# Preparing the last batch element's attention of a two-layer graph kernel: three blocks of Wh and half of the maxima moved beside the normalizing of its last block

## The chip, the cores and the metric

The kernel runs on one core of one Trainium2 chip. The metric is the device time of one execution in microseconds (us), the median of several runs. The profiled execution is one more run, with its own time and its own span.

## The reference, cut to what matters

Two layers run one after the other on x, of shape (8, 2048, 256) in float32, with one 2048 x 2048 adjacency matrix.

- Layer 0 is attention with four heads over chunks of 256 keys: scores are clipped to -10 to 10, masked with the adjacency, and each chunk has its own softmax. Its output is projected, added to x and normalized, and the result is added to x and normalized again. Call that h.
- Layer 1 is graph attention: Wh = h W, s_i = Wh a1, s_j = Wh a2, e = leaky_relu(s_i + s_j) with slope 0.2, masked by the adjacency, a softmax over all 2048 keys, then the sum of Wh with these weights, an ELU, the addition of h and a normalization.

```python
s_i = Wh @ a1
s_j = Wh @ a2
e = jax.nn.leaky_relu(s_i[:, :, None] + s_j[:, None, :], negative_slope=LEAKY_ALPHA)
e = jnp.where(mask[None, :, :], e, -jnp.inf)
attention = jax.nn.softmax(e, axis=-1)
h_prime = jnp.einsum('bij,bjo->bio', attention, Wh)
```

The layer-1 softmax of a query needs the largest score among its neighbours before any weight of that query can be made. As the slope is positive, it is enough to know the largest s_j among the neighbours.

## The kernel before, in words

The program is one instruction stream per engine, in an order written out by hand. The eight batch elements are run one after the other through layer 0, each in four blocks of 512 queries (IB = 512, NIB = 4), and each block in eight chunks of 256 keys (NCH = 8). The outer loop runs over all of these chunks (index J); each J has two halves, and each half is a **beat**. There are total = B * NIB * NCH = 256 chunks, so the loop's last score is made in beat 511, and beats 512 and 513 finish its products. Batch elements are numbered 0 to 7, and (7,3) is the last block of the last one. After the loop a short loop of its own goes on with beats until nothing is left (lines 782 to 786). This stretch is the **tail**.

A beat has three parts:

- begin_beat takes the layer-1 steps onward. A step is 128 keys against the 512 queries of one block; a block has 16 steps, a batch element four blocks. A step is *low* on ScalarE (L524) in one beat, *leaky* (L528) and *edges* (L533, with the mask) on VectorE in the next, *weights* (the exp, L537, on ScalarE, and for all but the last batch element an accumulate on GpSimd, L544 and L546) and *product* (TensorE, L556, or L571 for the last batch element) in the one after. A credit decides how many steps begin in a beat: 1.5 in the loop, 1.1 for its last batch element, 1.0 in the tail. The steps come strictly in order, so a batch element's first step cannot begin before the last step of the batch element ahead of it.
- Scores and context products of layer 0 stand in the middle. The last scaling of a context (L750 on VectorE, L751 on GpSimd) comes two beats after the product that it belongs to.
- end_beat issues the products, and then resumes each generator of two lists once: `ahead` (the preparation of layer 1, function prelude) and `fins` (fin after a layer-0 block, fin1 after a layer-1 block). Each `yield` ends a generator's turn in that beat.

fin normalizes a block of layer 0 over some ten beats: x loaded; two GpSimd additions; three beats later the output projection (L331), VectorE's addition (L338) and the first statistics (L292 to L295, and a power on GpSimd, L296); L301 and L303 normalize; GpSimd multiplies and adds (L343, L344); second statistics; second normalizing and the store of h; transposes (L356) into hT, which is stored too. For the last block of the last batch element, (7,3), the context is complete in beat 514, the projection is in beat 515, the second statistics in 518 and the transposes in 520. fin1 of the block of layer 1 ahead of it runs in the same beats (L486 and L487 in 519, its statistics in 520).

prelude(b) waits until all four blocks of batch element b have been normalized, loads hT back, makes Wh in one beat per block (L391 on TensorE, L394 on ScalarE), takes the columns s_j and s_i (L399 to L401), turns s_j into a row and spreads it over all partitions through DRAM (L406 to L412), and then makes the maxima. `far` is a matrix in DRAM, made at the start, that is 0 for a neighbour and hugely negative elsewhere. For each 128 queries and each half of the keys, L432 on VectorE adds s_j and a block of far (128 x 1024, 256 KB, loaded by L420 through two buffers) and takes the maximum: 32 such instructions per batch element. After eight of them, five small operations (L446 to L450) make the bounds for a block of 512 queries, which are transposed and spread through DRAM (L453 to L463). A block may start two beats after that.

All DMAs are issued by SP in one stream; an SP instruction that waits for a buffer holds back those behind it. The last batch element's Wh and key row use the buffers of kT and v, which layer 0 no longer needs. The product of the last batch element's layer 1 lies in the two PSUM buffers of the scores (ps_s).

Of the kernel before, what the change touches and what calls it, by code (L numbers as in the profile page):

```python
# [9 lines left out]
F32 = mybir.dt.float32  # L10
BF16 = mybir.dt.bfloat16
# [3 lines left out]
ALU = mybir.AluOpType  # L15
# [4 lines left out]
P = 128  # L20
CLIP = 10.0
EPS = 1e-5
SLOPE = 0.2
FAR = -(2.0**127)
# [4 lines left out]
def tile_adj_attention__then__gat(  # L29
# [35 lines left out]
    nc = tc.nc  # L65
    B, N, F = x.shape
    H, D = 4, 64
    CHUNK = 256
    KC = F // P
    NT = N // P  # L70
    IB = 512
    NIB = N // IB
    TPB = IB // P
    NPAIR = H // 2
    NCH = N // CHUNK
    DH = D // 2
    HT = NT // 2
    HN = N // 2
# [4 lines left out]
    dram3 = ctx.enter_context(tc.tile_pool(name="dram3", bufs=3, space=DRAM))  # L83
    ps_s = ctx.enter_context(tc.tile_pool(name="ps_s", bufs=2, space=PSUM))
    ps_u = ctx.enter_context(tc.tile_pool(name="ps_u", bufs=1, space=PSUM))
    ps_m = ctx.enter_context(tc.tile_pool(name="ps_m", bufs=2, space=PSUM))
    one = ctx.enter_context(tc.tile_pool(name="one", bufs=1))
    two = ctx.enter_context(tc.tile_pool(name="two", bufs=2))
    three = ctx.enter_context(tc.tile_pool(name="three", bufs=3))
    four = ctx.enter_context(tc.tile_pool(name="four", bufs=4))  # L90
# [221 lines left out]
    fin_near = [0] * B  # L312
    fins = []

    def fin(b, ib, ctxT):
# [37 lines left out]
        for k in range(KC):  # L353
# [1 line left out]
            for t in range(TPB):  # L355
                nc.tensor.transpose(pt[:, t, :], y[:, t, ts(k, P)], ident)  # L356
            nc.scalar.copy(hT[:, k, :], pt.rearrange("p t c -> p (t c)"))
        nc.sync.dma_start(out=hT_d[b, ib], in_=hT)


    blocks_done = 0

    def prelude(b):

        st = states[b]
        last = b == B - 1
        while fin_near[b] < NIB:
            yield  # L370
        hts = []

        def ht_load():
            ib = len(hts)
            if ib < NIB:
                t = four.tile([P, KC, IB], F32, tag="xT", name=f"hTl{b}_{ib}")
                nc.sync.dma_start(out=t, in_=hT_d[b, ib])
                hts.append(t)

        ht_load()  # L380
        ht_load()
        yield
        yield
        while not (last or blocks_done == b * NIB):
            yield
        wh = one.tile([P, NT, F + 2], F32, tag="kT" if last else "wh", name=f"wh{b}")
        for ib in range(NIB):
            for t in range(TPB):
                pw = ps_m.tile([P, F + 2], F32, tag="m", name=f"pw{b}_{ib}_{t}")
                for k in range(KC):  # L390
                    nc.tensor.matmul(  # L391
                        pw, hts[ib][:, k, ts(t, P)], W_aug[:, k, :], start=(k == 0), stop=(k == KC - 1)
                    )
                nc.scalar.copy(wh[:, ib * TPB + t, :], pw)  # L394
            ht_load()
            yield

        sj = two.tile([P, 3, NT], F32, tag="sj", name=f"sj{b}")
        nc.vector.tensor_copy(sj[:, 0, :], wh[:, :, F + 1])  # L399
        nc.vector.tensor_scalar_mul(sj[:, 1, :], wh[:, :, F + 1], SLOPE)  # L400
        nc.vector.tensor_copy(sj[:, 2, :], wh[:, :, F])  # L401
        if last:
            nc.vector.memset(wh[:, :, F : F + 1], 1.0)
        yield
        pt = ps_m.tile([NT, P], F32, tag="m", name=f"psj{b}")
        nc.tensor.transpose(pt, sj[:, 0, :], ident)  # L406
        rows = two.tile([NT, P], F32, tag="rows", name=f"sjr{b}")
        nc.scalar.copy(rows, pt)
        sj_d = dram3.tile([NT, P], F32, tag="sj_d", name=f"sj_d{b}")
        nc.sync.dma_start(out=sj_d, in_=rows)  # L410
        sj_row = one.tile([P, N], F32, tag="v" if last else "sj_row", name=f"sj_row{b}")
        nc.sync.dma_start(out=sj_row, in_=sj_d.rearrange("r c -> (r c)").partition_broadcast(P))  # L412
        st["wh"], st["sj"] = wh, sj
        fbs = []

        def fb_load():
            n = len(fbs)
            if n < 2 * NT:
                fb = two.tile([P, HN], BF16, tag="fb", name=f"fb{b}_{n}")
                nc.sync.dma_start(out=fb, in_=far[n // 2, n % 2])  # L420
                fbs.append(fb)

        fb_load()
        fb_load()
        yield
        yield
        for ib in range(NIB):

            mx = two.tile([P, TPB], F32, tag="mx", name=f"mx{b}_{ib}")
            m2 = two.tile([P, 2, TPB], F32, tag="m2", name=f"m2{b}_{ib}")  # L430
            for n in range(2 * TPB):
                nc.vector.tensor_tensor_reduce(  # L432
                    out=fbs[2 * TPB * ib + n],
                    in0=sj_row[:, ts(n % 2, HN)],
                    in1=fbs[2 * TPB * ib + n],
                    scale=1.0,
                    scalar=2 * FAR * 0.999,
                    op0=ALU.add,
                    op1=ALU.max,
                    accum_out=m2[:, n % 2, n // 2 : n // 2 + 1],  # L440
                )
                fb_load()
                if ib or n % 2:
                    yield
            s_i = sj[:, 2, ts(ib, TPB)]
            nc.vector.tensor_max(mx, m2[:, 0, :], m2[:, 1, :])  # L446
            nc.vector.tensor_add(mx, mx, s_i)
            nc.vector.scalar_tensor_tensor(mx, mx, SLOPE, mx, ALU.mult, ALU.max)
            nc.vector.tensor_sub(m2[:, 0, :], s_i, mx)
            nc.vector.scalar_tensor_tensor(m2[:, 1, :], s_i, SLOPE, mx, ALU.mult, ALU.subtract)  # L450
            yield
            pt = ps_m.tile([2 * TPB, P], F32, tag="m", name=f"pab{b}_{ib}")
            nc.tensor.transpose(pt, m2.rearrange("p n t -> p (n t)"), ident)  # L453
            rows = two.tile([2 * TPB, P], F32, tag="rows", name=f"abr{b}_{ib}")
            nc.scalar.copy(rows, pt)
            ab_d = dram3.tile([2 * TPB, P], F32, tag="ab_d", name=f"ab_d{b}_{ib}")
            nc.sync.dma_start(out=ab_d, in_=rows)
            yield

            while blocks_done < b * NIB + ib - 1:  # L460
                yield
            ab = two.tile([P, 2, IB], F32, tag="ab", name=f"ab{b}_{ib}")
            nc.sync.dma_start(  # L463
                out=ab.rearrange("p n q -> p (n q)"),
                in_=ab_d.rearrange("r c -> (r c)").partition_broadcast(P),
            )
            st["ab"][ib] = (beat + 2, ab)

    def fin1(b, ib, hx, acc):

# [25 lines left out]
            nc.scalar.activation(hx[:, t, :], us[t], AF.Identity, bias=ones[:, 0:1], scale=r[:, t : t + 1])  # L496

    states = [{"ab": {}} for _ in range(B)]

    def layer1():  # L500

# [89 lines left out]

    l1 = layer1()
    l1_live = True
    ahead = [prelude(b) for b in range(B)]
    lows, edged, weighted = [], [], []
    agenda = {}
    beat = 0
# [35 lines left out]
    def end_beat():  # L633

        nonlocal weighted
        for s in weighted:
            s.product()
        weighted = []
        for gens in (ahead, fins):
            for g in list(gens):  # L640
                if next(g, g) is g:
                    gens.remove(g)
        for fn in agenda.pop(beat, []):
            fn()
# [13 lines left out]

    prev = None
    v = None  # L660
    total = B * NIB * NCH
    mk0 = {}
    for J in range(total + 1):
        b, ib, j = J // (NIB * NCH), J // NCH % NIB, J % NCH
# [166 lines left out]
```

## Time and profile before

| what | value |
| --- | --- |
| median of 3 runs | 4443.78 us (4443.62 to 4454.05) |
| profiled execution, own time | 4445.93 us |
| its span | 4444.1 us |
| TensorE busy | 4076.1 us (92%) |
| VectorE busy | 3405.3 us (77%) |
| ScalarE busy | 2603.7 us (59%) |
| GpSimd busy | 1776.4 us (40%) |
| DMA over the span | mean 98 GB/s |
| span from the last scores' end to the kernel's end | about 4140 to 4444 us |

How to read it: the span is the time from the first to the last instruction of the profiled execution; shares are averages over stages with different limits. PE is TensorE, PEld its weight loads, DVE VectorE, ACT ScalarE, POOL GpSimd, SP the engine that issues DMAs. PEclk is the granted clock of TensorE as a share of full speed. A row such as "L432 ... 1.22" is a duration, and what stands in square brackets is the idle time of that engine ahead of the instruction and what ended it. A VectorE row that is longer than its fellows of the same shape was held up while it ran.

### The profile page before, as it was taken

What the parts mean: (1) busy time and instruction counts of PE and PEld (TensorE: products, weight loads), DVE (VectorE), ACT (ScalarE), POOL (GpSimd) and SP (SyncE); (2) the same over time, 40 slices, a digit from 0 to 9 for tenths busy, and PEclk for the clock granted to TensorE, in tenths of its full rate; (3) what the DMA queues carried; (4) which work ended last, traced back from release to release, by engine and by line L of the source; (5) the groups of instructions that cost most, each with busy time, mean ns of one, the idle gap of its engine ahead of it and who ended that gap; (6) DMA issues with size and microseconds to landing.
All of it is one profiled execution on the core that took longest, in us unless ns stands there. A gap on an engine that the chain in (4) does not pass through costs nothing. (4 is left out here: it accounts for less than half of the span.)

```text
span 4444.1 us, 61341 instructions
## 1 busy us (share of the span) xinstructions
PE 4076.1 (92%) x23052; PEld 1914.3 (43%) x23052; DVE 3405.3 (77%) x4527; ACT 2603.7 (59%) x3877; POOL 1776.4 (40%) x906
## 2 busy tenths in 40 slices
PE   7888999999899998999999999999989999899767
PEld 3222334444344543445334453444434444344545
DVE  4777469985799758996599866998579975898686
ACT  4665445665556655665556655666555665566445
POOL 0222224553355423554345542455325553355411
PEclk9999999999999999999999999999999999999988
DMA  4554333332322323323333223332232232332241
GB/s 149 167 164 152 92 100 101 96 93 78 105 81 91 101 64 115 89 77 92 99 99 91 78 77 104 101 101 86 84 101 87 86 103 68 118 92 73 65 136 54
DMA packets 266874, 433.98 MB, mean 98 GB/s; under 512 B 86097, under 2 KB 121169, under 8 KB 265553
## 3 DMA queue, kind: packets, MB, share of 16 engines
q1 hardware_dynamic: 266576, 430.06, 31.7%
q8 instruction: 181, 2.97, 0.3%
q14 instruction: 117, 0.95, 0.1%
HBM read 358.48 MB, written 69.40 MB: 96 GB/s over the span
## 5 line engine op out<-in xcount | busy, mean ns | idle before, releaser
L702 ACT ACTIVATE e<-sc 128x1024 f32<-128x1024 f32 x1024 | 1037.3, 1022 | 1146.7 <-DVE sc L699 1102.2
L699 DVE SCALAR_TENSOR_TENSOR sc<-sc,mk 128x1024 f32<-128x1024 f32 x1024 | 1205.8, 1222 | 512.8 <-PE sc L689 282.9
L689 PE MATMUL sc<-qT,kT 64*128 64x512 f32 x4096 | 1060.0, 632 | 106.9 <-ACT e L702 104.0
L751 POOL TENSOR_TENSOR ctxT<-ctxT,un 128x1024 f32<-128x1024 f32 x224 | 562.7, 2512 | 1164.1 <-DVE un L750 1059.1
L715 PE MATMUL u<-e,v 128*32 128x512 f32 x8192 | 980.4, 596 | 0.0
L556 PE MATMUL us<-wh,w 128*128 128x256 f32 x3584 | 875.5, 393 | 78.1 <-ACT w L537 60.5
L556 PEld LDWEIGHTS us<-wh,w 128*128 128x128 f32 x3584 | 662.8, 192 | 420.7 <-ACT w L537 117.7
L546 POOL TENSOR_TENSOR acc<-acc,w 128x512 f32<-128x512 f32 x392 | 602.7, 1537 | 541.0 <-ACT w L537 531.3
L689 PEld LDWEIGHTS sc<-qT,kT 64*128 64x128 f32 x4096 | 346.1, 188 | 627.4 <-ACT e L702 307.4
L528 DVE SCALAR_TENSOR_TENSOR w<-ab,sj,w 128x512 f32<-128x512 f32 x512 | 584.0, 1161 | 32.1 <-ACT w L524 32.1
L715 PEld LDWEIGHTS u<-e,v 128*32 128x32 f32 x8192 | 239.8, 110 | 657.7 <-issue 539.2
L533 DVE TENSOR_TENSOR w<-w,mk 128x512 f32<-128x512 f32 x512 | 475.1, 948 | 44.4 <-DMA mk<-mask 41.7
L715 PE MATMUL u<-e,ones 128*32 128x512 f32 x4096 | 498.3, 604 | 0.0
L432 DVE CUSTOM_DVE_ANT_0 fb<-sj_row,fb 128x1024 bf16<-128x1024 f32 x256 | 397.1, 1559 | 5.9 <-DMA fb<-far 5.6
L537 ACT ACTIVATE w<-w 128x512 f32<-128x512 f32 x512 | 310.7, 631 | 90.0 <-DVE w L533 89.6
L524 ACT ACTIVATE w<-ab,sj 128x512 f32<-128x512 f32 x512 | 353.3, 716 | 13.5 <-PE us L571 6.3
L750 DVE TENSOR_TENSOR un<-un,r 128x1024 f32<-128x1024 f32 x224 | 276.5, 1234 | 85.4 <-DMA r<-rd 78.8
L723 ACT COPY un<-u 128x512 f32<-128x512 f32 x512 | 300.6, 587 | 55.4 <-PE u L715 53.7
L715 PEld LDWEIGHTS u<-e,ones 128*32 128x32 f32 x4096 | 107.9, 110 | 359.5 <-issue 317.9
L737 DVE RECIPROCAL dc<-dc 128x16 f32<-128x16 f32 x256 | 64.1, 250 | 184.5 <-DMA dc<-ds 159.7
L571 PE MATMUL us<-wh,w 128*128 128x257 f32 x512 | 128.7, 413 | 45.9 <-ACT w L537 45.7
L487 POOL TENSOR_TENSOR hx<-hx,hr 128x1024 f32<-128x1024 f32 x32 | 91.6, 2862 | 191.6 <-DVE hx L486 191.6
(97 smaller groups left out, 3150.7 us busy)
## 6 DMA issues: line engine op xcount, KB each, us to landing
r<-rd SPq DMA_DIRECT2D x256, 256.0 KB
fb<-far SPq DMA_DIRECT2D x256, 256.0 KB
mk<-mask SPq DMA_DIRECT2D x120, 512.0 KB
xT_k<-in_xT_dram SPq DMA_DIRECT2D x32, 512.0 KB
raw<-in_adjT_dram SPq DMA_DIRECT2D x32, 512.0 KB
xT_q<-in_xT_dram SPq DMA_DIRECT2D x32, 512.0 KB
rawf<-in_adj_dram SPq DMA_DIRECT2D x32, 512.0 KB
xT_v<-in_xT_dram SPq DMA_DIRECT2D x32, 512.0 KB
```

The costliest lines, as they stand in the source:

```text
L432: nc.vector.tensor_tensor_reduce(out=fbs[2 * TPB * ib + n], in0=sj_row[:, ts(n % 2, HN)], in1=fbs[2 * TPB * ib + n], scale=1.0, scalar=2 * ...
L524: nc.scalar.activation(self.w, k["ab"][:, 1, :], AF.Identity, bias=k["sj"][:, 1, c : c + 1])
L528: nc.vector.scalar_tensor_tensor(self.w, k["ab"][:, 0, :], k["sj"][:, 0, c : c + 1], self.w, ALU.add, ALU.max)
L533: nc.vector.tensor_tensor(self.w, self.w, self.k["mks"][self.c // HT][:, self.c % HT, :], ALU.min)
L537: nc.scalar.activation(self.w, self.w, AF.Exp)
L546: nc.gpsimd.tensor_add(k["acc"], k["acc"], self.w)
L556: nc.tensor.matmul(k["us"][:, t, :], self.w[:, ts(t, P)], k["wh"][:, c, 0:F], start=(first and t % 2 == 0), stop=last, skip_group_check=True,)
L689: nc.tensor.matmul(sc[:, h, :], kT[h * D : (h + 1) * D, hp, ts(c, P)], qT[h * D : (h + 1) * D, hp, :], start=True, stop=True,)
L699: nc.vector.scalar_tensor_tensor(scs[hp], scs[hp], -CLIP, cap, ALU.max, ALU.min)
L702: nc.scalar.activation(e, scs[hp], AF.Exp)
L715: nc.tensor.matmul(m[h * DH : (h + 1) * DH, :], prev["v"][:, pc, f0 : f0 + DH] if part < 2 else ones[:, 0:DH], prev["es"][2 * i + h // 2][ ...
L751: nc.gpsimd.tensor_add(p["ctxT"], p["ctxT"], p["un"])
```

## The change

For batch elements 0 to 6 the preparation issues the same instructions as before; it is only cut into functions. For the last one a generator of its own, last_prelude, takes its place:

- At beat 2*total - 4 (508) it loads hT of the three blocks that are ready.
- In beats 512, 513 and 514 it makes Wh of these three blocks. In 513 it also takes the key columns of the first half (blocks 0 and 1); in 514 it spreads their row and loads far for eight of the sixteen groups of 128 queries whole, 512 KB each, into the eight buffers of the layer-0 exponentials (tag "e"), which are free by then.
- In beats 515 to 519 it issues three maxima a beat over the first half of the keys, until fin has made the last hT.
- In beat 520 it makes Wh of the last block straight from fin's tile (which is no longer stored and loaded back), the key columns and the row of the second half. The sixteenth maximum over the first half and those over the second half follow, four of them in one beat for block 0, then one a beat. Groups 8 to 15 come through the two far buffers as before.
- A block may start one beat after its bounds are spread, where it was two.
- From beat 2*total on, end_beat resumes fins before ahead.

```diff
-        nc.sync.dma_start(out=hT_d[b, ib], in_=hT)
+        if (b, ib) == (B - 1, NIB - 1):
+            states[b]["hT"] = hT
+        else:
+            nc.sync.dma_start(out=hT_d[b, ib], in_=hT)
...
+    def key_columns(wh, sj, r):
+        nc.vector.tensor_copy(sj[:, 0, r], wh[:, r, F + 1])
+        nc.vector.tensor_scalar_mul(sj[:, 1, r], wh[:, r, F + 1], SLOPE)
+        nc.vector.tensor_copy(sj[:, 2, r], wh[:, r, F])
+
+    def key_rows(b, sj, sj_row, r):
+        n = r.stop - r.start
+        pt = ps_m.tile([n, P], F32, tag="m", name=f"psj{b}_{r.start}")
+        nc.tensor.transpose(pt, sj[:, 0, r], ident)
+        rows = two.tile([n, P], F32, tag="rows", name=f"sjr{b}_{r.start}")
+        nc.scalar.copy(rows, pt)
+        sj_d = dram3.tile([n, P], F32, tag=f"sj_d{n}", name=f"sj_d{b}_{r.start}")
+        nc.sync.dma_start(out=sj_d, in_=rows)
+        nc.sync.dma_start(
+            out=sj_row[:, r.start * P : r.stop * P], in_=sj_d.rearrange("r c -> (r c)").partition_broadcast(P)
+        )
...
+    def last_prelude(b):
+        st = states[b]
+        while beat < 2 * total - 4 or fin_near[b] < NIB - 1:
+            yield
+        hts = [load_hT(b, ib) for ib in range(NIB - 1)]
+        while beat < 2 * total:
+            yield
+        wh = one.tile([P, NT, F + 2], F32, tag="kT", name=f"wh{b}")
+        sj = two.tile([P, 3, NT], F32, tag="sj", name=f"sj{b}")
+        wh_block(b, wh, hts[0], 0)
+        yield
+        wh_block(b, wh, hts[1], 1)
+        halves = [slice(0, HT), slice(HT, NT)]
+        key_columns(wh, sj, halves[0])
+        yield
+        sj_row = one.tile([P, N], F32, tag="v", name=f"sj_row{b}")
+        key_rows(b, sj, sj_row, halves[0])
+        wh_block(b, wh, hts[2], 2)
+        held = []
+        for it in range(HT):
+            fr = eight.tile([P, N], BF16, tag="e", name=f"far{b}_{it}")
+            nc.sync.dma_start(out=fr.rearrange("p (n w) -> p n w", n=2), in_=far[it].rearrange("n p w -> p n w"))
+            held.append(fr)
+        fbs, fb_load = far_loads(b, [(it, hf) for hf in range(2) for it in range(HT, NT)])
+        yield
+        m2 = one.tile([P, NIB, 2, TPB], F32, tag="m2l", name=f"m2{b}")
+
+        def half(it, hf):
+            fb = held[it][:, ts(hf, HN)] if it < HT else fbs.pop(0)
+            half_max(sj_row, fb, hf, m2[:, it // TPB, hf, it % TPB : it % TPB + 1])
+            if it >= HT:
+                fb_load()
+
+        firsts = list(range(NT))
+        while "hT" not in st:
+            for it in firsts[:3]:
+                half(it, 0)
+            firsts = firsts[3:]
+            yield
+        wh_block(b, wh, st["hT"], NIB - 1)
+        key_columns(wh, sj, halves[1])
+        nc.vector.memset(wh[:, :, F : F + 1], 1.0)
+        key_rows(b, sj, sj_row, halves[1])
+        st["wh"], st["sj"] = wh, sj
+        yield
+        while firsts:
+            half(firsts.pop(0), 0)
+        for ib in range(NIB):
+            for t in range(TPB):
+                half(ib * TPB + t, 1)
+                if ib:
+                    yield
+            less_max(sj, ib, m2[:, ib], f"{b}_{ib}")
+            ab_d = query_rows(m2[:, ib], f"{b}_{ib}")
+            yield
+            while blocks_done < b * NIB + ib - 1:
+                yield
+            st["ab"][ib] = (beat + 1, query_bc(ab_d, f"{b}_{ib}"))
...
-    ahead = [prelude(b) for b in range(B)]
+    ahead = [prelude(b) for b in range(B - 1)] + [last_prelude(B - 1)]
...
-        for gens in (ahead, fins):
+        for gens in (ahead, fins) if beat < 2 * total else (fins, ahead):
```

wh_block, load_hT, far_loads, half_max, less_max, query_rows and query_bc hold the instructions of lines 387 to 467 unchanged.

## The prediction

> **What bounds the kernel now.** Read first: the page's 40 slices. TensorE fills 0.9 of nearly every slice; only the last three are slack, and in two of them the granted clock drops too.
>
> ```profile
> PE   7888999999899998999999999999989999899767
> DVE  4777469985799758996599866998579975898686
> PEclk9999999999999999999999999999999999999988
> ```
>
> A slice is 111 us, so this is from about 4111 us on. All that the change moves lies there; before beat 508 it issues the same instructions. Second: busy time by stage, cut at the landmarks of that tail.
>
> ```profile
> core 0: us, PE busy (x) PEld busy (x) DVE busy (x) ACT busy (x) POOL busy (x), PEclk, DMA share, GB/s
> 4140.30:4155.40 15.10, 10.99 (x50) 7.60 (x50) 14.28 (x9) 5.04 (x10) 12.66 (x6) 0.89 0.32 87
> 4155.40:4185.90 30.50, 16.62 (x65) 13.56 (x64) 20.88 (x34) 13.34 (x23) 17.58 (x11) 0.78 0.11 36
> 4185.90:4221.40 35.50, 26.80 (x115) 21.36 (x113) 14.64 (x27) 15.42 (x34) 9.01 (x7) 0.95 0.25 88
> 4221.40:4233.50 12.10, 9.53 (x41) 7.41 (x41) 7.32 (x6) 5.45 (x10) 7.05 (x5) 1.00 0.37 133
> 4233.50:4250.20 16.70, 8.26 (x24) 5.54 (x24) 15.94 (x21) 2.50 (x4) 4.58 (x3) 0.76 0.36 110
> 4250.20:4269.30 19.10, 1.92 (x10) 1.83 (x10) 11.43 (x30) 9.12 (x16) 5.18 (x2) 0.50 0.41 142
> 4269.30:4306.30 37.00, 32.03 (x129) 24.90 (x129) 35.10 (x62) 18.49 (x31) 0.00 (x0) 0.95 0.46 149
> 4306.30:4349.90 43.60, 32.44 (x128) 26.66 (x129) 38.06 (x73) 24.68 (x43) 4.19 (x2) 0.88 0.34 114
> 4349.90:4389.20 39.30, 31.79 (x130) 26.10 (x129) 28.33 (x46) 24.46 (x41) 4.19 (x2) 0.91 0.20 73
> ```
>
> The rows are: end of the last scores to the first output projection (beats 512 to 515); normalizing of block (7,3), up to its transposes (515 to 520); reload and the four Wh blocks (520 to 525); key rows (526 to 528); the eight maxima of block 0 (529 to 532); the bare stall until batch 7's first product (TensorE busy 1.9 of 19.1); then blocks 0, 1 and 2 of batch 7. In beats 520 to 539 TensorE waits for a chain, which the chain view gives in order of time:
>
> ```profile
> 4216.91 3.50 PE pw L391 x16
> ...
> 4225.54 1.34 DMA sj_d<-sjr
> ...
> 4227.32 6.08 DMA fb<-far
> ...
> 4248.18 2.16 DVE fb L432
> ```
>
> So the chain can be shortened. The other thing to see is what VectorE's two-input operations do beside GpSimd, in the timeline:
>
> ```profile
> 4168.83 2.80 POOL L343 TENSOR_TENSOR y<-y,gamma_bc 128x1024 f32<-128x1024 f32 x1
> 4169.46 2.72 DVE L533 TENSOR_TENSOR w<-w,mk 128x512 f32<-128x512 f32 x1
> ...
> 4243.05 1.46 POOL L546 TENSOR_TENSOR acc<-acc,w 128x512 f32<-128x512 f32 x1 [3.28 <-ACT w L537]
> ...
> 4243.52 2.07 DVE L432 CUSTOM_DVE_ANT_0 fb<-sj_row,fb 128x1024 bf16<-128x1024 f32 x1
> ```
>
> The L533 row takes 0.69 elsewhere, the maximum (L432) 1.22: each ends only after GpSimd's operation did. I therefore add such VectorE work and GpSimd's work up as if they were one engine; an accumulate (L546) beside them costs 2.07 - 1.22 = 0.85.
>
> **The change part by part.** Durations are those of the profiled run (span 4444.1, own time 4445.93). A pair leaky + edges (L528, L533) is 0.74 + 0.69 = 1.43; three maxima are 3.66.
>
> *Three Wh blocks in beats 512 to 514.* 16 matmuls of a block took 3.6. TensorE's queue from the end of beat 512's product at 4140.3: Wh 3.6, context part 1.9, product 1.9, Wh 3.6, bubble 1.0, product 1.9, key transpose 0.3, Wh 3.6, bubble 1.0, two products 3.8: 4162.9. The bubble is the exp queued on ScalarE behind the last Wh copy (each product of beats 523 to 525 sat 0.99 for it). The output projection started at 4155.4, so it is 7.5 late. A new wait, VectorE's key_columns at the end of beat 513, holds the leaky and edges of 514 and the last context scaling (L750) until about 4152.3; L750 and its GpSimd add (L751) then end near 4159.7, hidden by the 4162.9 above. If the Wh blocks were free, that wait alone would cost 5.6 (L751 ended at 4154.1).
>
> *First-half maxima in beats 515 to 519, three a beat.* They stand on VectorE after this beat's normalizing step and before the next one.
> - Statistics a end at 4162.0 + 7.5 = 4169.5. Three maxima and one pair come before L301: it ends at 4174.8 (before: 4164.8).
> - From there to statistics b: six maxima 7.3, two pairs 2.9, GpSimd's multiply and add 2 x 2.37 (its row without VectorE beside it, 4137.70), two accumulates 1.7. Sum 16.6, so 4191.4 (before: 4174.4).
> - Statistics b 2.4; three maxima 3.7; one wait of 1.7, because far blocks 8 to 15 still go through two buffers (a load needs about 3 us from release, by the 0.33 wait at 4238.98); pair 1.4, L301 0.2; block (6,2)'s L486 1.2 and L487 2.4; three maxima 3.7; pair and accumulate 2.3. Statistics c (those of block (6,2)), 4185.9 before, start at 4210.4: 24.5 late. The transposes and Wh block 3 run beside this on TensorE (about 4206 to 4212), hidden by VectorE; uncovered they would cost 3.6.
>
> *Reload and key row.* The store and reload of hT, and with them the four beats of 6.5 at 4195 to 4221, go away. After statistics c (2.4): key_columns 0.5, transpose and copy 0.8, store 1.4, half a key row 3.7. The last is not in the trace; the whole row and two far blocks took 6.08, half the row alone cannot beat the store's 1.34. I take 3.7, nearer the first. VectorE waits in beat 521, with batch 6's steps queued behind. Then four maxima, an accumulate and less_max, 4.9 + 0.85 + 0.85: 4225.8.
>
> *Batch 6's own steps.* One a beat, the last is issued in beat 531, so batch 7 starts at beat 532 at the earliest, not fourteen beats sooner (it started in 537). Beats 522 to 525 hold a pair, a maximum and an accumulate, 3.5 each, 14.0; 526 takes 3.1; 527 to 532 2.25 each (five products from 4221.4 to 4232.4), 13.5; the pair of 533 and an exp 2.0. First product of batch 7: 4258.4, before 4269.3. **Gain 10.9.**
>
> *Blocks of batch 7.* fin1 of block (6,3) lay in the stall (beats 533 to 537), now inside block 0. Block 2, with a fin1 and no maxima, took 39.3; block 1, with eight maxima, 43.6: 0.54 each. Block 0: 39.3 + 4 x 0.54 = 41.5 against 37.0, a loss of 4.5. Block 1 has four maxima fewer, 2.2, and its mask load is no longer queued on SP behind far loads (0.92 at 4305.65): a gain of 3.1. Net loss 1.4.
>
> *Queues.* At beat 508 three hT loads (1.5 MB) pass the small reciprocal transfers; the spread of beat 508 was issued at 4119.7 and used at 4125.8, so I cost it at nothing, and at 2 at most. At beat 514 eight loads of 512 KB and two of 256 KB pass on SP in front of the mask of block (6,3), 5.2 MB with it. In 4228.5 to 4231.5 the DMA engines moved 393 GB/s, in 4227.5 to 4229.5 262: 13 to 20 us from 4157, when the first half's key row has left SP. The mask is there by 4177, its edges come at about 4180. Cost nothing.
>
> Sum: 10.9 - 1.4 = 9.5. The profiled execution would go from 4445.93 to 4436.4; the median of before is 2.15 below that execution, so **4434.3**.
>
> By the Trainium skill, "SBUF — State Buffer", section "Who interferes with whom", a VectorE instruction with two SBUF inputs and a GpSimd instruction that reads SBUF exclude each other for a whole instruction, and issue order decides who waits. The 2.72 and 2.07 rows agree. It speaks against this change. Taken at its worst, each accumulate costs its full 1.27 instead of 0.85, some 20 accumulates between 4150 and 4258 take 8 more, and the gain shrinks to about 1; the sum above goes by the rows.
>
> **The rivals.** *The maxima hide after all (faster).* VectorE was busy 20.9 of the 30.5 between 4155.4 and 4185.9, so 9.6 is idle, 4.1 of it in waits after 4164 for ScalarE and GpSimd. If maxima fill those and GpSimd's work costs no extra (the 16.6 becomes VectorE's own 10.2, L487 gives back 2.4), and fin1 of (6,3) is covered in block 0 (4.5), the gain is 9.5 + 6.4 + 2.4 + 4.5 = 22.8: 4421. Against it: the stretched rows. With beats 527 to 532 at TensorE's 1.92 instead of 2.25 and no late start at the reciprocals it reaches 4419.
>
> *The mask waits for the held blocks (slower).* One queue, 5.2 MB ahead. At the 110 GB/s of the stage that fetched far blocks (4233.5 to 4250.2) the mask lands at 4157 + 47 = 4204, VectorE stands 24 at the edges of (6,3)'s first step with all normalizing behind it, and 9.5 gained becomes 14.5 lost: 4458. Below 226 GB/s it begins to cost, below 160 it decides the sign. For it: the mean rate. Against it: that stage asked for two blocks at a time, ten at once should run at the 262 to 393 rows.
>
> *Nothing is gained.* If far blocks 10 to 15 wait 1.2 each more (7) and the half row takes 6.08 (2.4), the sum is zero: 4444, inside the forecast's class.
>
> **How the numbers follow.** 0.3% is 13.3 us, about what a measurement of this kernel can tell from no change: faster means below 4430.4. The forecast with its unknowns, 4431 to 4446, has 0.57; hidden maxima 0.36; the late mask 0.07. The range, 4416 to 4450, takes the forecast, the faster case with 3 to 5 us to spare, and the start of the slow one.
>
> **What would show it.** Right: output projection near 4163, statistics b near 4191, statistics c near 4210, batch 7's first product near 4258, its blocks 0 and 1 both near 41.5, and stretched L432 rows beside L343, L344 and L487. Wrong: statistics c before 4203 (maxima hidden), or an L533 wait on the mask of several us in beat 517 (the queue), or a first product before 4250.

## The result, and the profile after

The changed kernel took 4437.49 us, the median of 12 runs (4431.34 to 4441.82); the kernel before, on the same chip, 4443.70 (12 runs, 4438.14 to 4454.05). The ratio is 0.9985, 95% interval [0.9976, 0.9994]: the medians are 6.2 us apart, a small gain, since the interval does not reach 1, and well inside the 0.3% that the prediction counts as no change. The profiled execution took 4440.12 (span 4438.3), before 4445.93 (4444.1).

One thing has to be known before two profiles are laid side by side. The main loop has the same instructions in both up to beat 508, yet its end shifts by several us from execution to execution. The last group of score matmuls started at 4129.1 before and at 4131.5 after. (It ended at 4131.1 before; the 4140.3 that the text ahead calls the end of the last scores is the end of beat 512's product.) So all that follows counts from that start, and *tail* means the time from there to the end of the span: 315.0 before, 306.8 after. The tail is 8.2 shorter, the loop happened to be 2.4 longer, and 5.8 is what the two profiled executions differ by. A tail, too, is read from one execution: block 2 of batch 7, which has the same steps in all these kernels, took 37.2 to 39.3 us in their profiles. Differences of tail under 2 us or so are therefore not read as effects.

The page's slices, as before: TensorE, VectorE, granted clock.

```profile
PE   7888999999899999999989999999989999899767
DVE  4776468985799758996599966898569975898786
PEclk9999999999999999999999999999999999999889
```

At 111 us a slice hardly anything is to be seen; the last three TensorE digits are the same 767. The stages show it. Each row is a stretch, its length, the busy time of five engines with their instructions, the granted clock, and what the DMA engines did: end of beat 512's product to the output projection; projection to the GpSimd addition of block (6,2); from there to the bounds of block 0; batch 6's last steps to batch 7's first product; then blocks 0, 1 and 2 of batch 7.

```profile
core 0: us, PE busy (x) PEld busy (x) DVE busy (x) ACT busy (x) POOL busy (x), PEclk, DMA share, GB/s
4142.70:4164.65 21.95, 19.96 (x98) 15.23 (x97) 11.75 (x12) 11.02 (x24) 13.80 (x8) 1.00 0.29 91
4164.65:4208.35 43.70, 18.97 (x66) 14.55 (x65) 38.23 (x61) 13.02 (x22) 18.82 (x10) 0.69 0.43 159
4208.35:4225.30 16.95, 7.11 (x34) 5.18 (x32) 14.73 (x36) 6.04 (x13) 3.26 (x3) 0.89 0.34 109
4225.30:4261.20 35.90, 25.87 (x99) 19.65 (x99) 34.94 (x42) 16.62 (x29) 19.43 (x12) 0.91 0.17 59
4261.20:4305.10 43.90, 34.76 (x137) 28.59 (x137) 31.78 (x57) 25.12 (x43) 5.18 (x2) 0.84 0.26 84
4305.10:4346.80 41.70, 33.68 (x129) 27.28 (x129) 33.35 (x60) 24.70 (x43) 5.14 (x2) 0.84 0.26 89
4346.80:4384.70 37.90, 30.36 (x128) 25.05 (x128) 28.23 (x47) 24.59 (x42) 4.19 (x2) 0.95 0.16 56
```

The bare stall of before (TensorE busy 1.9 of 19.1 us) is gone: in the 35.9 that take its place TensorE has 25.9. But VectorE is now the engine without a gap: 38.2 of 43.7 beside the normalizing, 34.9 of 35.9 beside batch 6's steps, and TensorE pays there, with 19.0 of 43.7 (before, 16.6 of 30.5 over the normalizing, and 26.8 of 35.5 over the reload and the Wh blocks). The stall moved forward.

The timeline of VectorE and GpSimd says why VectorE is so full. First while (7,3) is normalized, then in beats 522 to 525:

```profile
4181.84 2.79 POOL L343 TENSOR_TENSOR y<-y,gamma_bc 128x1024 f32<-128x1024 f32 x1
4182.46 2.72 DVE L620 TENSOR_TENSOR w<-w,mk 128x512 f32<-128x512 f32 x1
4184.71 2.68 POOL L344 TENSOR_TENSOR y<-y,x 128x1024 f32<-128x1024 f32 x1
4185.10 3.37 DVE L412 CUSTOM_DVE_ANT_0 far<-sj_row,far 128x1024 bf16<-128x1024 f32 x1
...
4235.54 1.45 POOL L633 TENSOR_TENSOR acc<-acc,w 128x512 f32<-128x512 f32 x1 [2.08 <-ACT w L624]
4235.79 1.75 DVE L615 SCALAR_TENSOR_TENSOR w<-ab,sj,w 128x512 f32<-128x512 f32 x1
4237.58 0.69 DVE L620 TENSOR_TENSOR w<-w,mk 128x512 f32<-128x512 f32 x1
4238.19 1.22 DVE L412 CUSTOM_DVE_ANT_0 far<-sj_row,far 128x1024 bf16<-128x1024 f32 x1
```

(L412 is the maximum in the new numbering, L615 leaky, L620 the edges, L633 the accumulate, L624 the exp, L573 the last addition of fin1.) An edges operation that takes 0.69 took 2.72, and a maximum of 1.22 took 3.37. Both started while a GpSimd operation ran and ended after it: the edges 0.55 after the multiply (L343), the maximum 1.08 after the addition (L344). That is a little less than their own time, as if each had run only when GpSimd was done. From one accumulate to the next, beats 522 to 525 are 3.54 apart (4235.54 to 4239.08): pair 1.43, maximum 1.22, accumulate 0.85 make 3.50. That these agree so well is partly luck: without its accumulate the same beat takes 2.53 (below), so VectorE's own parts come to less than their sum of 2.65, and the accumulate to 1.01.

Two more rows answer to the two waits that the prediction priced: a far load through two buffers, and the half key row.

```profile
4198.55 2.36 DVE L412 CUSTOM_DVE_ANT_0 fb<-sj_row,fb 128x1024 bf16<-128x1024 f32 x1 [1.71 <-DMA fb<-far]
```

The first is VectorE's wait in the timeline, 1.71; the second is the half key row in the chain of waits, 3.86 from its issue:

```profile
4215.91 3.86 DMA sj_row<-sj_d
```

### The profile page after: what moved, and what is told of

Read it like the earlier page. It is cut to its first block, busy times and chain, and to the rows that moved or that the text cites. A ratio compares the mean times of both kernels' runs of the same rounds, so it can differ in the third digit from the quotient of the medians.

```text
span 4438.3 us, 61328 instructions
## 1 busy us (share of the span) xinstructions
PE 4076.7 (92%) x23053; PEld 1913.9 (43%) x23053; DVE 3412.6 (77%) x4530; ACT 2604.1 (59%) x3878; POOL 1782.7 (40%) x906
## 5 line engine op out<-in xcount | busy, mean ns | idle before, releaser
L643 PEld LDWEIGHTS us<-wh,w 128*128 128x128 f32 x3584 | 663.9, 192 | 416.6 <-ACT w L624 110.6
L633 POOL TENSOR_TENSOR acc<-acc,w 128x512 f32<-128x512 f32 x392 | 607.8, 1551 | 528.6 <-ACT w L624 512.7
L615 DVE SCALAR_TENSOR_TENSOR w<-ab,sj,w 128x512 f32<-128x512 f32 x512 | 587.6, 1168 | 15.4 <-ACT w L611 15.3
L620 DVE TENSOR_TENSOR w<-w,mk 128x512 f32<-128x512 f32 x512 | 467.8, 934 | 42.9 <-DMA mk<-mask 40.0
L412 DVE CUSTOM_DVE_ANT_0 fb<-sj_row,fb 128x1024 bf16<-128x1024 f32 x240 | 383.8, 1608 | 2.4 <-DMA fb<-far 2.4
L624 ACT ACTIVATE w<-w 128x512 f32<-128x512 f32 x512 | 310.5, 631 | 66.3 <-DVE w L620 64.9
L573 POOL TENSOR_TENSOR hx<-hx,hr 128x1024 f32<-128x1024 f32 x32 | 91.6, 2862 | 177.8 <-DVE hx L572 177.8
```

Source lines behind the costliest of these rows:

```text
L412: nc.vector.tensor_tensor_reduce(out=fb, in0=sj_row[:, ts(hf, HN)], in1=fb, scale=1.0, scalar=2 * FAR * 0.999, op0=ALU.add, op1=ALU.max, a ...
L615: nc.vector.scalar_tensor_tensor(self.w, k["ab"][:, 0, :], k["sj"][:, 0, c : c + 1], self.w, ALU.add, ALU.max)
L620: nc.vector.tensor_tensor(self.w, self.w, self.k["mks"][self.c // HT][:, self.c % HT, :], ALU.min)
L624: nc.scalar.activation(self.w, self.w, AF.Exp)
L633: nc.gpsimd.tensor_add(k["acc"], k["acc"], self.w)
L643: nc.tensor.matmul(k["us"][:, t, :], self.w[:, ts(t, P)], k["wh"][:, c, 0:F], start=(first and t % 2 == 0), stop=last, skip_group_check=True,)
```

## The experiments

All are read from the last score group on (us). "Start" is the first product of batch 7. In the four kernels that have no accumulates in (6,3) it is the end of that block's reciprocals, marked *, some 1.7 us ahead of that product (4236.05 and 4237.72 in the one with all three edits).

The expectations name absolute times against the changed kernel's 4437.5. The first four experiments ran on another chip, on which the kernel before took 4435.75 instead of 4443.70, and the changed kernel was not run there. So tails and ratios are compared below, and an absolute time that meets its expectation proves little. The changes of tail and of the median against the kernel before agree within some 2.5 us in all of them but the last, where the loop itself grew.

| kernel | last scores | projection | statistics b | statistics c | start | tail |
| --- | --- | --- | --- | --- | --- | --- |
| before | 4129.1 | 26.2 | 45.3 | 56.8 | 140.1 | 315.0 |
| changed | 4131.5 | 33.2 | 60.6 | 80.0 | 129.7 | 306.8 |
| first maxima later | 4118.8 | 33.2 | 52.2 | 64.3 | 126.9 | 307.4 |
| maxima and Wh later | 4119.6 | 27.9 | 49.6 | 61.2 | 123.8 | 304.4 |
| no accumulates for (6,3) | 4125.1 | 33.2 | 60.6 | 78.1 | 117.9* | 294.2 |
| far not held | 4118.8 | 33.2 | 64.2 | 83.3 | 136.9 | 314.3 |
| maxima and Wh later, no accumulates | 4133.7 | 26.7 | 48.4 | 59.2 | 110.6* | 289.9 |
| additions on VectorE | 4129.2 | 33.2 | 58.8 | 77.8 | 127.3 | 299.8 |
| the same, additions on VectorE: all three | 4126.2 | 25.9 | 43.2 | 57.3 | 109.8* | 284.7 |
| no accumulates, additions on VectorE | 4126.3 | 33.2 | 58.8 | 76.7 | 118.0* | 288.9 |
| more steps a beat | 4150.1 | 38.5 | 69.6 | 45.2 | 123.7 | 301.3 |

(With more steps a beat, the statistics of block (6,2) come ahead of statistics b.)

The theory was the prediction's: VectorE's two-input work and GpSimd's work add up, so what is put beside the normalizing is paid there, and the gain is only the reload and the stall. The rivals: the early maxima do hide; SP's queue delays the tail behind the held loads; the steps of batch 6 alone set the start.

### First-half maxima after the last block instead of beside it

```diff
-        fbs, fb_load = far_loads(b, [(it, hf) for hf in range(2) for it in range(HT, NT)])
+        fbs, fb_load = far_loads(b, [(it, hf) for it in range(HT, NT) for hf in range(2)])
...
-        while "hT" not in st:
-            for it in firsts[:3]:
-                half(it, 0)
-            firsts = firsts[3:]
-            yield
+        while "hT" not in st:
+            yield
...
+                for hf in range(2):
+                    half(ib * TPB + t, hf)
+                    if ib:
+                        yield
```

> The changed kernel without its first-half maxima in beats 515 to 519: the early Wh blocks, the early key row of the first half and the held far blocks stay, but all 32 maxima come after beat 520 (eight in beat 521 for block 0, then one a beat). Theory (maxima and GpSimd's work add up on the normalizing chain, nothing hides): the fifteen early maxima cost 15 x 1.22 = 18.3 there; given back are 3.7 (three more maxima in beat 521), 4.9 (four more beats with a maximum among batch 6's last steps) and 4.3 (eight more beats with a maximum in batch 7, 0.54 each), so the time is 5.4 us shorter than the changed kernel's 4437.5: about 4432; statistics c start near 4191, batch 7's first product near 4251 (landmarks of the changed profile 4211.5 and 4261.2). Rival (early maxima fill idle time of VectorE): they cost at most 9 on the chain, and the kernel gets 4 to 12 us slower than the changed one: 4442 to 4450, first product at or after 4261.

Measured 4430.90 (11 runs) against 4435.75 for the kernel before on the same chip (25 runs): 0.9990 [0.9981, 0.9999]. Statistics c came 15.6 earlier, so the early maxima do not hide: they are paid while (7,3) is normalized. But the tail did not shorten; it is 0.6 longer than the changed kernel's. Of the 15.6, 12.8 are given back before batch 7's first product. Three more maxima for block 0 are 3.7; one maximum a beat in eight beats instead of four, among batch 6's last steps, is 4.9; and one wait is this:

```profile
4189.65 0.17 DVE L380 COPY sj<-wh 128x8 f32<-128x8 f32 x1 [4.06 <-ACT wh L371]
```

VectorE stands 4.06 for the last Wh block. The prediction had named this cover and priced it at 3.6; the expectation for this run forgot it. These three make 12.6. Blocks 0 and 1 of batch 7 then lose another 3.0 (45.3 and 43.3, against 43.9 and 41.7), with maxima of the first half now in them. The theory's mechanism stands and its sum for this run fell: early maxima are paid in full where they are and save as much later, so that this part of the change brings nothing that these runs can tell. (The 4430.90 lies near the 4432 that was expected only because this chip was the faster one.)

The mask is worth a look here. In this kernel no maxima stand between its load and the first edges of (6,3), and they wait for it:

```profile
4162.91 0.69 DVE L615 TENSOR_TENSOR w<-w,mk 128x512 f32<-128x512 f32 x1 [0.81 <-DMA mk<-mask]
```

The load landed 9.1 us after its issue at 4153.81, and 0.81 too late. So the prediction's rival of the late mask is real, if small, where the steps come early.

### The three Wh blocks two beats later as well

```diff
-        while beat < 2 * total:
-            yield
...
+        while beat < 2 * total + 2:
+            yield
...
+        for ib in range(NIB - 1):
+            wh_block(b, wh, hts[ib], ib)
+            yield
+        key_columns(wh, sj, halves[0])
+        key_rows(b, sj, sj_row, halves[0])
```

(added to the kernel above, the held loads ahead of the loop)

> As the run with all maxima after beat 520, and the three early Wh blocks moved from beats 512 to 514 into 515 to 517, behind the output projection in TensorE's queue; the first half's key columns and row come in beat 518. Theory: the Wh blocks and the key columns cost 7.5 on the path in beats 512 to 514 and nothing in 515 to 517, where TensorE is idle for some 14 of 30 us: another 7.5 shorter, about 12.9 below the changed kernel, 4424.6; output projection near 4157 (changed kernel: 4164.7). Rival (TensorE's late products hold the steps back wherever the blocks stand): no further gain, about 4432.

Measured 4425.78 (9 runs), 0.9973 [0.9963, 0.9983]. Against the kernel above, the projection came 5.2 earlier, but only 2.6 of it were left at statistics b, and the tail is 3.0 shorter; it is 2.4 below the changed kernel's, where 12.9 was expected. (The 4425.78 is near the expected 4424.6 by the faster chip alone.) VectorE's waits show where the rest stayed:

```profile
4162.85 1.32 DVE L608 SCALAR_TENSOR_TENSOR w<-ab,sj,w 128x512 f32<-128x512 f32 x1 [4.42 <-ACT w L604]
...
4169.16 0.43 DVE L292 BATCH_NORM_STATS2 st_b<-y 128x6 f32<-128x256 f32 x1 [2.24 <-POOL y L344]
```

Here the Wh blocks delay another queue. ScalarE's four copies of each Wh block follow its matmuls at 0.87 apart and stand ahead of the exp and the low (L604) of the next step, so the leaky waits 4.42, where it waited 1.11 in the kernel above. The wait of statistics b for GpSimd's addition is no new one: it was 2.24 in the kernel above, too, and 2.25 before. The Wh blocks cost less two beats later, not nothing.

### No accumulates in block (6,3)

Its products take the sums from a column of ones in Wh, as batch 7's do.

```diff
+    def ones_column(k):
+        return (k["b"], k["ib"]) >= (B - 2, NIB - 1)
...
-            if k["b"] == B - 1:
+            if ones_column(k):
...
+        if b == B - 2:
+            nc.vector.memset(wh[:, :, F : F + 1], 1.0)
```

> The changed kernel, with block (6,3) summed the way the last batch element is: its weights are summed by a column of ones in Wh, its product lies in the score buffers, and GpSimd's sixteen accumulates of that block are gone. Theory (GpSimd's accumulates block VectorE's two-input operations): beats 522 to 525 fall from 3.5 to about 2.65 us, 527 to 532 from 2.37 to about 2.0, three stretched operations in 519 to 521 give 3; minus about 4 for waiting on the score buffers at the start of batch 7; 5 to 9 us shorter than the changed kernel: 4429 to 4433, and L615 and L412 at 0.74 and 1.22 in beats 522 to 532. Rival (VectorE's long rows there have another cause, and TensorE's or ScalarE's steps set the beat): the beats stay at 2.4 and 3.5, and the time is 0 to 4 longer: 4437 to 4442.

Measured 4418.11 (5 runs), 0.9956 [0.9944, 0.9969]; the tail is 12.6 shorter than the changed kernel's, more than expected. GpSimd's instructions on the page went from 906 to 891: 15 accumulates (the expectation's sixteen was one too many); the sum by eight small matmuls at the block's end went too. In beats 522 to 525 nothing is stretched any more:

```profile
4222.95 1.22 DVE L412 CUSTOM_DVE_ANT_0 far<-sj_row,far 128x1024 bf16<-128x1024 f32 x1
4224.09 0.75 DVE L620 SCALAR_TENSOR_TENSOR w<-ab,sj,w 128x512 f32<-128x512 f32 x1
4224.87 0.69 DVE L625 TENSOR_TENSOR w<-w,mk 128x512 f32<-128x512 f32 x1
4225.48 1.22 DVE L412 CUSTOM_DVE_ANT_0 far<-sj_row,far 128x1024 bf16<-128x1024 f32 x1
```

(L620 and L625 are leaky and edges here.) A beat with a maximum is 2.53 instead of 3.54, so an accumulate costs 1.01 there, more than the prediction's 0.85 from one row. A beat without a maximum is 1.75 instead of 2.30, where the products follow each other on TensorE 1.73 apart: 0.55 is saved. Of the 12.6, statistics c have 1.9, and another 8.4 is gained from there to the last product of (6,3). The rest falls into block 0 of batch 7, where no accumulate stands; it presumably belongs to the other way in which this kernel ends block (6,3), which was not tried alone. So 10.3 is the most that the accumulates alone can have cost, 0.7 each on average. The expected size was too small mainly because it counted on losing 4 at the score buffers in block 0, where something was gained.

### The far blocks not held

```diff
-        for it in range(HT):
-            fr = eight.tile([P, N], BF16, tag="e", name=f"far{b}_{it}")
...
+        fbs, fb_load = far_loads(b, [(it, hf) for hf in range(2) for it in range(NT)])
```

> The changed kernel without the held far blocks: all 32 maxima take far through the two 256 KB buffers, first halves in beats 515 to 519 as in the changed kernel. Theory (a maximum through two buffers takes about 2.4 us where maxima follow each other): the nine maxima of beats 515 to 517 and the four of beat 521 wait 0.6 to 1.2 more each, 8 to 14 us longer than the changed kernel: 4445 to 4451. Rival 1 (the other work between the maxima hides the loads): within 3 us of 4437.5. Rival 2 (4.2 MB of held blocks on the one queue delay the mask and the first maxima): shorter than 4437.5 by several us.

Measured 4436.79 (11 runs), 1.0002 [0.9993, 1.0011]; the tail is 7.5 longer than the changed kernel's, just under the expected span; 1.45 of it is block 2 of batch 7, whose steps are the same (39.34 at a granted clock of 0.91, against 37.89 at 0.95), so some 6 are the loads'. It is not the queue: loads taken off it made the kernel slower. VectorE's waits are those of two buffers, once in each beat of three maxima:

```profile
4162.44 1.23 DVE L412 CUSTOM_DVE_ANT_0 fb<-sj_row,fb 128x1024 bf16<-128x1024 f32 x1 [1.51 <-DMA fb<-far]
...
4180.38 1.23 DVE L412 CUSTOM_DVE_ANT_0 fb<-sj_row,fb 128x1024 bf16<-128x1024 f32 x1 [2.28 <-DMA fb<-far]
```

Without the held blocks the change would be worth 0.7 of tail (315.0 to 314.3), which one profile of each can't tell from nothing; the ratio says the same.

### The additions on VectorE

From beat 512 on, GpSimd's 128 x 1024 operations (L343, L344, the addition of fin1, the context addition) go to VectorE.

```diff
-        nc.gpsimd.tensor_mul(y, y, bc_rows(gamma_bc))
-        nc.gpsimd.tensor_add(y, y, xt)
+        eng = nc.vector if beat >= 2 * total else nc.gpsimd
+        eng.tensor_mul(y, y, bc_rows(gamma_bc))
+        eng.tensor_add(y, y, xt)
```

> The changed kernel, with GpSimd's 128 x 1024 operations that are issued after the last score (the last context add, multiply and add of block (7,3), and the addition of h in each fin1) on VectorE instead; the accumulates stay. Theory (a GpSimd operation stops VectorE's two-input work for its whole time, so 2.37 there is worth as much as 2.37 on VectorE, where the same work takes 1.22): 2.3 less between statistics a and b, 1.2 in beat 519, about 1.4 in each of four blocks, 1.1 at the end: the tail of 306.8 becomes about 297, ratio near 0.9963. Rival (GpSimd works beside VectorE, and VectorE is the bound): five operations of 1.22 more on VectorE, tail 306 to 312, ratio 0.9985 to 0.9995.

Measured 4431.52 (6 runs) against 4444.26 (12 runs): 0.9971 [0.9960, 0.9982]. The tail is 299.8, 7.0 below the changed kernel's, where 297 was expected; the rival (306 to 312) is out. 2.4 of it comes before batch 7's first product and 4.6 behind it. The busiest engine of this stretch was given more work and the kernel became faster:

```profile
4180.73 1.22 DVE L344 TENSOR_TENSOR y<-y,gamma_bc 128x1024 f32<-128x1024 f32 x1
4181.99 1.23 DVE L345 TENSOR_TENSOR y<-y,x 128x1024 f32<-128x1024 f32 x1
4183.13 1.22 DVE L413 CUSTOM_DVE_ANT_0 far<-sj_row,far 128x1024 bf16<-128x1024 f32 x1
```

The same two operations took 2.79 and 2.68 on GpSimd, and VectorE was held meanwhile. Here they cost it 1.22 and 1.23, and the maximum behind them is back from 3.37 to 1.22.

By the Trainium skill, "SBUF — State Buffer", section "Who interferes with whom", a VectorE instruction with two SBUF inputs and a GpSimd instruction that reads SBUF exclude each other for a whole instruction. The trace agrees: the edges and the maximum are 2.72 and 3.37 beside the 2.79 and 2.68 on GpSimd, and 0.69 and 1.22 when GpSimd has no part in it. So do the tails, -7.0 and -12.6 us where GpSimd's work is taken away. The worst reading, a full 1.27 for each accumulate, is not what was measured: 1.01 beside a maximum, 0.55 without one.

### The versions in combination

No accumulates and Wh later:

> The three early Wh blocks in beats 515 to 517, all maxima after beat 520, and block (6,3) summed by a column of ones (no accumulates). Counted from the start of the last score group, the changed kernel's tail took 306.8, the kernel with later Wh blocks 304.4, the one without accumulates 294.2. Theory (the accumulates' cost lies in beats 522 to 533, where both kernels issue the same steps): the gains add, 12.6 less than 304.4 but for the 1.9 that the early maxima saved in beats 518 to 520: about 293.5, ratio near 0.995. Rival (the gain without accumulates came from the early maxima being free of them): about 300, ratio near 0.997.

Measured 4423.45 (6 runs), 0.9948 [0.9932, 0.9964], tail 289.9, 3.6 below the expectation. All three edits:

> Later Wh blocks, maxima after beat 520, no accumulates in block (6,3), and GpSimd's 128 x 1024 operations of the tail on VectorE. Theory: the tail of about 293.5 less another 9: 284 to 286, ratio near 0.993. Rival (one bound, TensorE's products in batch 7, is reached first): about 292, ratio 0.995.

Measured 4412.23 (6 runs), **0.9932 [0.9919, 0.9945]**, tail 284.7, as expected: 30 us below the kernel before, and the fastest version here. Its stages while (7,3) is normalized, while statistics c and Wh's last block are made, and from the key row to the end of block (6,3):

```profile
core 0: us, PE busy (x) PEld busy (x) DVE busy (x) ACT busy (x) POOL busy (x), PEclk, DMA share, GB/s
4152.13:4183.53 31.40, 24.39 (x105) 19.83 (x104) 19.54 (x41) 17.84 (x37) 5.01 (x4) 0.93 0.18 68
4183.53:4195.00 11.47, 9.69 (x42) 7.49 (x41) 5.05 (x18) 5.48 (x12) 1.01 (x1) 0.91 0.28 105
4195.00:4236.00 41.00, 25.67 (x101) 19.74 (x99) 35.43 (x69) 16.91 (x31) 0.00 (x0) 0.83 0.21 77
```

GpSimd has 0 of the 41.0 after the key row, and in the first row TensorE has 24.4 of 31.4 where the changed kernel gave it 19.0 of 43.7. To see whether the early maxima pay once GpSimd is out of the way, the last two edits alone, with the change's own order:

> The changed kernel with its early Wh blocks and early maxima, without accumulates in block (6,3), and with GpSimd's 128 x 1024 operations of the tail on VectorE. With GpSimd almost gone from the tail, early maxima cost only their own 1.22 each. Theory: 294.2 less some 9, 285, the same as the kernel with all maxima after beat 520 within 2. Rival (early maxima pay once nothing blocks them): 3 or more below that kernel.

Measured 4417.00 (5 runs), 0.9940 [0.9928, 0.9952], tail 288.9: 4.2 more than with all three, where no difference was expected. By the tails, moving the maxima and Wh forward loses a little even without GpSimd beside it. By the medians the two intervals overlap, and the 4.2 is one profiled execution of each, so that loss is not shown. The rival, a gain from the early maxima, doesn't show either.

### More steps a beat in the loop's last batch element

```diff
-    RATE, LAST_RATE = 1.5, 1.1
+    RATE, LAST_RATE = 1.5, 1.25
```

> The changed kernel with the credit of the last batch element's beats at 1.25 steps instead of 1.1, so that nine or ten of batch 6's steps move from the tail into the main loop. Theory (one step a beat of batch 6 holds batch 7's start at beat 532, while its bounds are ready at 523): batch 7 starts about nine beats earlier, the tail from the last score group falls from 306.8 to about 284 (three beats at 3.5, one at 3.1, five at 2.4, less four maxima that then lie in batch 7 at 0.54 each); the main loop, where TensorE is the bound, grows by 9.6 x 1.92 = 18.4; in sum 5 shorter, ratio near 0.9975. Rival (batch 7's start waits for its bounds): the tail falls by less than 5 and the sum is some 14 longer, ratio near 1.002.

Measured 4456.86 (6 runs) against 4443.90 (10 runs): 1.0032 [1.0020, 1.0044], slower. The loop ends 18.6 later, where 18.4 was expected; as loop ends vary by several us, so close an agreement is partly luck. The time from the transposes of (7,3) to batch 7's first product fell from 52.8 to 38.9, so batch 6's steps, one a beat, do hold that start. But only 5.6 of tail were won, close to the rival's figure, since fin1 of block (6,2) now falls in the middle of the Wh blocks. The first row waits for its sum on TensorE, the second for the copies of Wh that stand behind it:

```profile
4171.12 0.18 DVE L567 RECIPROCAL r<-pr 128x4 f32<-128x4 f32 x1 [4.92 <-PE pr L565]
...
4177.42 0.17 DVE L380 COPY sj<-wh 128x8 f32<-128x8 f32 x1 [6.12 <-ACT wh L371]
```

The first edges of (6,3), too, now wait for the mask, whose load stands behind the reciprocals' transfers:

```profile
4158.84 0.69 DVE L620 TENSOR_TENSOR w<-w,mk 128x512 f32<-128x512 f32 x1 [3.56 <-DMA mk<-mask]
```

The projection is 5.4 and statistics b 9.0 later than in the changed kernel. The expectation left out that the steps' rate also moves the fin1s.

## Why the prediction was right

The forecast was 4434.3, a change of less than the 0.3% that it set as its limit, and 4437.49 was measured. Its steps, counted from the last scores:

| step | predicted | measured |
| --- | --- | --- |
| output projection later | 7.5 | 6.9 |
| statistics b later | 17.0 | 15.3 |
| statistics c later | 24.5 | 23.2 |
| two-buffer wait for far | 1.7 | 1.71 |
| half key row | 3.7 | 3.86 |
| batch 7 starts earlier | 10.9 | 10.4 |
| block 0 loses | 4.5 | 6.7 |
| block 1 gains | 3.1 | 2.7 |
| block 2 gains | 0 | 1.4 |
| tail shorter | 9.5 | 8.2 |

(block 3 and the end give the other 0.4.)

- **The rule that work adds up** carried the sum and is shown from two sides, by the accumulates taken out and by the additions moved to VectorE. Its price of 0.85 an accumulate was a middle: 1.01 was measured beside a maximum, where the prediction used it, and 0.55 without one. In the sum for beats 522 to 525 the error is made up for by VectorE's own work, which took a little less than its parts. The rival of hidden maxima is refuted by the 15.6 that statistics c gains without them. What the prediction did not see is that they were worth nothing either: it counted what they cost in the normalizing and what the whole path gains, never the maxima alone.
- **The term that was mis-sized** is fin1 of (6,3) in block 0: 4.5 was worked out from blocks 1 and 2 of before, and 6.7 was measured. In block 0 fin1's addition meets VectorE's two-input work:

```profile
4268.87 3.26 POOL L573 TENSOR_TENSOR hx<-hx,hr 128x1024 f32<-128x1024 f32 x1 [9.52 <-DVE hx L572]
4269.86 2.83 DVE L615 SCALAR_TENSOR_TENSOR w<-ab,sj,w 128x512 f32<-128x512 f32 x1
...
4268.11 8.02 PE L658 MATMUL us<-wh,w 128*128 128x257 f32 x24 [4.14 <-ACT w L624]
```

  The leaky is 2.83 for 0.74, the addition 3.26 for 2.34 (its row at the end of the kernel), and TensorE, one product into block 0, had already waited 4.14 for an exp that stood behind fin1's steps. But blocks 1 and 2 of before, from which the price was taken, have a fin1 too, with edges of 2.72 beside an addition of 2.73 and 2.74; so this meeting alone doesn't explain the 2.2 above the price. With the additions on VectorE block 0 takes 42.16 for 43.92, so up to 1.8 of the 6.7 are GpSimd's (the granted clock was 0.88 instead of 0.84 there, which has its part in it). Some of the 6.7 is in TensorE's own work, which no step counted: its busy time in the block went from 32.0 to 34.8, of which 1.0 is the eight small matmuls of (6,3)'s sum; the granted clock, in the rows of the two stages, went from 0.95 to 0.84. TensorE's idle time grew by the other 4. How the clock and the waits divide it was not tried.
- **Block 2's 1.4** was in no step. The waits are the same to 0.01 in both profiles; its last twelve products took 24.02 before and 22.62 after, at a granted clock of 0.88 and 0.93 in these two stretches. That points at the clock and not at the steps; why the clock differed was not tried. So there is luck in the sum: without this 1.4 the tail would be 6.8 shorter and not 8.2 (the medians say 6.2). It makes up for most of what block 0 lost beyond its 4.5.
- **The queue** cost nothing in the changed kernel: the first edges of (6,3) had no wait on the mask, and without the held loads the kernel lost time. The late mask did not come, but the margin is small: issued at 4166.60, and taking the 9.1 us that it took with all maxima later, it was there at about 4176 (an estimate), and the edges came at 4182.46, held back by the maxima. In the kernels with earlier edges it cost 0.81 and 3.56.
- **Wh of the last block** was hidden, as said; where its cover was taken away it cost 4.06 against the 3.6 named.
- **Batch 6's one step a beat** as the cap of batch 7's start is supported by the 13.9 that a higher rate saved behind the transposes, in a kernel that was slower as a whole; no kernel here gains by it.

## What to carry to other kernels

Where VectorE bounds a stretch, GpSimd's operations that read SBUF beside it are no free second engine: add their time to VectorE's two-input work, and try the same operation on VectorE, where the 128 x 1024 operations cost about half (1.22 for 2.3 to 2.8) in this case. Work that is moved forward into such a stretch is paid there; before crediting the gap that it leaves behind, name what covers the rest of that gap (here a Wh block of 4 us and the steps of the batch ahead). And compare two profiles from a common landmark close to the change, not from time zero.

## What was not expected of the hardware

- The identical main loop ended between 4118.8 and 4133.7 in the ten profiles that share its schedule, a spread of 14.9 us, nearly twice the change's own effect, with no difference in instructions until beat 508 but for a small memset in four of them. Part of it goes with the chip: the first four kernels ran on one (4118.8 to 4125.1; kernel before 4435.75 in the median), the next four on another (4126.2 to 4133.7; 4444.26).
- A whole operation moved from GpSimd to VectorE, the busiest of that stretch, saved time: 2.79 + 2.68 became 1.22 + 1.23.
- The granted clock differed over the same block with the same waits (0.91 and 0.95 in block 2), beside 1.4 us in twelve products. What set it is open.
